# Transformer block on one core: tile 15's first output-projection half moved ahead of tiles 13 and 14's feed-forward, a last sum in 256 columns, and a fused last scaling

## The chip, the core and the metric

The kernel runs on one core of a Trainium2 chip. A core has a matrix engine (TensorE, PE in the profile), three engines for element-wise work (VectorE or DVE, ScalarE or ACT, GpSimd or POOL) and SyncE (SP), which here issues the data transfers. Each engine takes its instructions in the order of the program; engines wait for each other by semaphores. The metric is the device time of one execution in microseconds; several executions are timed and the median is given.

## The reference

One attention layer and one feed-forward layer with routed low-rank adapters, in float32, for 4 sequences of 512 tokens and 1024 features:

```python
x = x + layernorm(attention(layernorm(x)))       # 32 heads of 32, 8 KV heads, RoPE, causal
x = x + layernorm(feed_forward(layernorm(x)))

# end of attention:      out @ w_o.T + b_o
# feed_forward(h):       h @ base_w.T + base_b + 2 * sum over 2 of 8 experts of
#                        weight_e * (h @ lora_A[e].T) @ lora_B[e].T
# layernorm(v):          (v - mean(v)) / sqrt(var(v) + 1e-5), over the 1024 features
```

## The kernel before

**Tiles.** The 2048 tokens are 16 tiles of 128. Tiles are worked in the order 0 to 11, 13, 14, 15, 12, in pairs; the last pairs are (13, 14) and (15, 12). For a pair, a 1024x1024 projection is done by a seven-block Strassen form (`seven`, acc_q, acc_o, acc_f for q, o and f): seven blocks of four matmuls of 128x512, with sums of the two tiles' inputs (s_q, s_o, s_f) made on VectorE and GpSimd. The last pair's o and f are done a tile at a time by `whole`: for each half of 512 output columns, eight matmuls sum into one PSUM bank (f adds a ninth, the low-rank part, which reads lowT). Each weight block of 128x512 is a "piece" of 256 KB, loaded by SP into a ring of 13 (`bring_pieces`, L489); a slot is free again when all uses of its piece are done.

**A tile's way.** Attention: scores (sc), their maximum (nmax), exponentials (pr), scaling (pr by rtot, GpSimd), transposes (pt_p to prT), weighted values (av to aT). Then o of a tile: acc_o plus the bias into w (VectorE), bn_stats of each half (L511), aggregate (mv), veps, then on GpSimd rstd (L527, a power) and shift (L531, -mean x rstd); w is scaled by ScalarE or VectorE (L552, L546), added to y (the residual, loaded from x) and y is normed once more into w (`attended`). w is transposed (pt_h, L577, to T_h). T_h goes into the gate and low-rank product (acc_gl, L602) and into f; `gate` ranks the eight experts in a chain of small VectorE instructions, which ends in low, its transpose pt_low (L1224) and lowT. After f, `finished` takes w's statistics by halves, scales w, adds it to y and stores y (L1264). There are two y buffers: tile 15's y is loaded (L865) when tile 13's output has landed, tile 12's after tile 14's.

**Order.** The program does not leave the order to the hardware: a planner (`Order`) replays the kernel with a cost for each operation and writes every engine's instruction order. TensorE's lanes are scores, transposes, values and three dense lanes; in the dense lane `main_lane` projections stand in the order in which the code puts them there. At the end of the list:

```python
for n, pair in enumerate(pairs[:-1]):
    out_of(pair)
    if n + 2 < len(pairs):
        q_of(pairs[n + 2])
    ffn_of(pair)
for tok in pairs[-1]:
    out_of([tok])
for tok in pairs[-1]:
    ffn_of([tok])
```

So o of (13, 14) is followed by their f, then o of 15, o of 12, f of 15, f of 12. Between o and f of (13, 14) stand, on TensorE, the two tiles' transposes and gates and the last attention group of tile 12.

Of the kernel before, what the change touches and what calls it, by code (L numbers as in the profile page):

```python
# [16 lines left out]
P = 128  # L17
# [74 lines left out]
class Order:  # L92
# [173 lines left out]
def kernel(  # L266
# [228 lines left out]
    class Norm:  # L495


        def __init__(self, name, urgent):
            self.name, self.urgent = name, urgent
            self.stats = None  # L500

        def half(self, src, h):
            if self.stats is None:
                self.stats = small.tile(
                    [P, NH, 6], F32, tag="stats", bufs=4, name=f"stats_{self.name}"
                )
            cols = slice(h * 512, (h + 1) * 512)
            yield dve(
                0.69,
                self.urgent,  # L510
                lambda: nc.vector.bn_stats(out=self.stats[:, h, :], in_=src()[:, cols]),  # L511
            )

        def scale(self):
            name = self.name

            def aggr():
                self.mv = small.tile([P, 2], F32, tag="mv", bufs=4, name=f"mv_{name}")
                nc.vector.bn_aggr(out=self.mv, in_=self.stats)

            def eps():
                self.veps = small.tile([P, 1], F32, tag="veps", bufs=4, name=f"veps_{name}")
                nc.vector.tensor_scalar_add(self.veps, self.mv[:, 1:2], EPS)  # L523

            def root():
                self.rstd = small.tile([P, 1], F32, tag="rstd", bufs=4, name=f"rstd_{name}")
                nc.gpsimd.tensor_tensor(out=self.rstd, in0=self.veps, in1=neg_half, op=ALU.pow)  # L527

            def shift():
                self.shift = small.tile([P, 1], F32, tag="shift", bufs=4, name=f"shift_{name}")  # L530
                nc.gpsimd.tensor_scalar(  # L531
                    self.shift, self.mv[:, 0:1], self.rstd, -1.0, ALU.mult, ALU.mult
                )

            yield dve(0.2, self.urgent, aggr)
            yield dve(0.15, self.urgent, eps)
            yield pool(0.6, 0, root)
            yield pool(0.4, 0, shift)

        def apply(self, dst, src, h):  # L540
# [51 lines left out]
    def project(lhsT, w, n, name, needs, take):  # L592


        acc = []
        steps = []

        def issue(c):
            if not acc:
                acc.append(ps.tile([P, 512], F32, tag="ps", name=f"acc_{name}"))  # L600
            last = c == len(needs) - 1
            nc.tensor.matmul(  # L602
                acc[0][:, :n], lhsT=lhsT(c), rhs=w(c), start=(c == 0), stop=last
            )
            if last:
                start(take(acc[0], steps_of[c].done), order.now)

        for c in range(len(needs)):
            us = 0.858 if n == 512 else 0.24
            steps.append(Step(us, partial(issue, c), needs[c], bank=(c == 0)))  # L610
        steps_of = list(steps)
        return steps
# [4 lines left out]
            start(piece.used(step.done))  # L617
        return steps

    def whole(name, tok_name, k, lhsT, ready, take, room, used=None, more=None):  # L620

        used = used or block(name, plain, 0, k) + block(name, plain, 1, k)
        needs = [[ready[c // 4], used[c].here] for c in range(ND)]
        needs[0] += room
        if more:
            needs.append(more[2])
        return with_pieces(
            used,
            project(
                lambda c: lhsT()[:, c, :] if c < ND else more[0](),  # L630
                lambda c: used[c].sb if c < ND else more[1],
                512,
                f"{name}_{tok_name}_{k}",
                needs,
                take,
            ),
        )
# [608 lines left out]
    def finished(tok):  # L1246

        t = tok.t
        norm = Norm(f"4_{t}", 3)
        halves = [Task() for _ in range(NH)]  # L1250
        added, out_halves = [Task() for _ in range(NH)], [Task() for _ in range(NH)]

        def ended(h):
            yield from norm.half(lambda: tok.w, h)
            halves[h].finish(order.at)

        def out_half(h):
            yield from norm.apply(lambda: tok.w, lambda: tok.w, h)
            yield from add_half(lambda: tok.y, lambda: tok.w, h, 2, tok.last)
            added[h].finish(order.at)  # L1260
            cols = slice(h * 512, (h + 1) * 512)
            yield sp(
                0.7,
                lambda: nc.sync.dma_start(  # L1264
                    out=out[t * P : (t + 1) * P, cols], in_=tok.y[:, cols]
                ),
            )
            yield LANDS
            out_halves[h].finish(order.at)

        def rest():
            yield halves
            yield from norm.scale()
            for h in range(NH):
                start(out_half(h), order.at)
            yield added
            w_slots.give(order.at)
            yield out_halves
            y_slots.give(order.at)

        start(rest())
        return ended

    def ffn(pair):

        ended = [finished(tok) for tok in pair]

        def to(k, h):
            return pair[k].w[:, h * 512 : (h + 1) * 512]

        def free(k, at):
            hT_slots.give(at)

        def lowT(k):
            return lambda: pair[k].lowT

        lo, hi = wlora_sb[:, :512], wlora_sb[:, 512:D]
        if len(pair) == 2:
            a, b = pair
            d, has_d = [], Task()  # L1300

            def difference():
                yield [a.low_done, b.low_done]
                d.append(small.tile([P, P], F32, tag="lowTd", bufs=1, name=f"lowTd_{a.t}"))
                yield dve(0.2, 1, lambda: nc.vector.tensor_sub(d[0], a.lowT, b.lowT))
                has_d.finish(order.at)
# [20 lines left out]
        tok = pair[0]  # L1327

        def take(h, acc, done):
            yield done  # L1330
            if h == NH - 1:
                free(0, order.at)
            cols = slice(h * 512, (h + 1) * 512)
            yield dve(0.69, 0, lambda: nc.vector.tensor_add(to(0, h), acc, bbase_sb[:, cols]))
            banks.give(order.at)
            yield from ended[0](h)

        steps = []
        for h in range(NH):
            steps += whole(  # L1340
                "f",
                tok.t,
                h,
                tok.hT_tile,
                tok.h_ready,
                partial(take, h),
                [],
                more=(lowT(0), (lo, hi)[h], [tok.low_done, loaded["lora"]]),
            )
        return steps  # L1350
# [269 lines left out]
    def out_of(pair):  # L1620
        main_lane.extend(attention_out(pair))
# [15 lines left out]
        for steps in products:  # L1637
            main_lane.extend(steps[k * ND : (k + 1) * ND])
    q_of(pairs[1])
    for n, pair in enumerate(pairs[:-1]):  # L1640
        out_of(pair)
        if n + 2 < len(pairs):
            q_of(pairs[n + 2])
        ffn_of(pair)
    for tok in pairs[-1]:
        out_of([tok])
# [80 lines left out]
```

## Time and profile before

| | us |
|---|---|
| median of 3 runs (1186.48 to 1186.75) | 1186.6 |
| the profiled execution | 1187.52 |
| its span in the trace | 1185.7 |
| TensorE busy, of the span | 1145.5 (97%) |
| VectorE busy | 823.9 (69%) |
| mean granted TensorE clock | 0.994 of full |

The span is the time from the first to the last instruction in the trace; the rest of an execution's time lies around it. A row of a timeline gives start, busy time, engine, line, operation, result<-inputs, shapes and count. TensorE's matmuls are pipelined: a row's busy time has about 0.15 us of a last matmul's way through the array in it, so the pace is read from one start to the next. TensorE's idle time by who ended it, from 1060 us on (us in total, times, longest):

```profile
PE pt_h L577 <- DVE rtot L1422: 5.9, 1, 5.9
PE acc_f L602 <- ACT lowT L335: 0.4, 1, 0.4
PE pt_low L1224 <- DVE low L1212: 0.4, 1, 0.4
PE acc_o L602 <- DMA piece<-in_w_o_dram: 0.3, 1, 0.3
```

### The profile page before, as it was taken

The numbers are of one execution on the slowest core, as the hardware profiler recorded it, in microseconds if no ns is written. First come the engines' busy times: TensorE is split into PE (matmuls) and PEld (weight loads), VectorE is DVE, ScalarE is ACT, GpSimd is POOL, SyncE is SP. The second block draws the span as 40 slices with busy tenths as digits, with TensorE's granted clock in tenths as the row PEclk, the third lists the DMA queues.
The fourth block names the chain that finished last, engine by engine and source line by source line (L and its number), as shares of the span: only waits on it lengthen the run. The fifth ranks groups of instructions, "written<-read, shape, count | busy, mean of one in ns | idle before, by whom it ended". The sixth has DMA issues, their size and how long they took to land.

```text
span 1185.7 us, 21412 instructions
## 1 busy us (share of the span) xinstructions
PE 1145.5 (97%) x7248; PEld 627.0 (53%) x7248; DVE 823.9 (69%) x1609; ACT 533.1 (45%) x1555; POOL 608.0 (51%) x857
## 2 busy tenths in 40 slices
PE   7999999999999999999999999999999999998996
PEld 3445545555556555565545555556655555545443
DVE  4687877875778756787667775678866786675353
ACT  0355544555555345454524334456543554552010
POOL 2575866553656536456455444545544564544221
PEclk9999999999999999999999999999999999998998
DMA  9869768434672636635377344762457645573883
GB/s 347 292 233 350 248 216 264 152 124 152 218 253 74 195 119 226 206 108 174 120 244 244 126 160 143 226 210 81 161 179 244 214 134 164 168 267 110 284 303 110
DMA packets 118315, 232.52 MB, mean 196 GB/s; under 512 B 13504, under 2 KB 14528, under 8 KB 118208
## 3 DMA queue, kind: packets, MB, share of 16 engines
q1 hardware_dynamic: 118208, 231.16, 59.0%
q8 instruction: 58, 0.95, 0.3%
q14 instruction: 49, 0.40, 0.1%
HBM read 210.14 MB, written 20.97 MB: 195 GB/s over the span
## 4 chain that ended last, share of the span: by engine, by line
PE 80%; DVE 8%; DMA 4%; POOL 4%; ACT 2%; issue 1%; SPq 0%; POOLq 0%; ACTq 0%; DVEq 0%
PE acc_f L602 19%; PE acc_o L602 15%; PE acc_q L602 11%; PE pt_p L1467 11%; PE acc_kv L602 7%; PE sc L1372 6%; PE av L1490 6%; PE acc_gl L602 2%; DVE nmax L1451 2%; POOL pr L1407 2%; ACT pr L1393 1%; PE pt_h L577 1%; DVE sc L1441 1%; DMA mix_o<-in_w_o_dram 1%; PE pt_q L996 1%
## 5 line engine op out<-in xcount | busy, mean ns | idle before, releaser
L1407 POOL TENSOR_SCALAR pr<-pr,rtot 128x256 f32<-128x256 f32 (+3 forms) x512 | 303.9, 610 | 249.3 <-DVE rtot L1422 183.9
L1393 ACT ACTIVATE pr<-sc,nmax 128x256 f32<-128x256 f32 (+3 forms) x512 | 264.6, 537 | 108.7 <-DVE nmax L1451 60.8
L1451 DVE TENSOR_REDUCE nmax<-sc 128x2 f32<-128x768 f32 (+3 forms) x176 | 198.2, 1126 | 32.6 <-ACT pr L1393 28.7
L1467 PE MATMUL pt_p<-ident,pr 128*128 128x128 f32 x1280 | 174.2, 276 | 3.5 <-POOL pr L1407 1.6
L1467 PEld LDWEIGHTS pt_p<-ident,pr 128*128 128x128 f32 x1280 | 144.1, 141 | 61.4 <-issue 46.5
L335 ACT COPY prT<-pt_p 128x512 f32<-128x512 f32 (+1 forms) x264 | 135.2, 548 | 83.6 <-PE pt_p L1467 82.9
L1441 DVE TENSOR_TENSOR sc<-sc,cmask 128x256 f32<-128x256 f32 (+2 forms) x176 | 96.7, 549 | 41.0 <-PE sc L1372 35.0
L602 PE MATMUL acc_kv<-wkv_sb,T_xn 128*128 128x512 f32 x256 | 119.4, 600 | 0.0
L335 ACT COPY aT<-av 128x128 f32<-128x128 f32 (+2 forms) x82 | 25.6, 312 | 195.0 <-PE av L1490 195.0
L1393 ACT ACTIVATION_READ_ACCUMULATOR pr<-sc,nmax 128x1 f32 x512 | 108.9, 213 | 0.0
L602 PE MATMUL acc_f<-piece,T_h 128*128 128x512 f32 x232 | 108.7, 596 | 0.0
L602 PE MATMUL acc_o<-piece,aT 128*128 128x512 f32 x232 | 106.3, 595 | 0.5 <-DMA piece<-in_w_o_dram 0.3
L602 PE MATMUL acc_q<-piece,s_q 128*128 128x512 f32 x224 | 105.1, 597 | 1.2 <-DVE raw_q L713 0.9
L602 PE MATMUL acc_o<-piece,s_o 128*128 128x512 f32 x224 | 103.4, 593 | 0.7 <-PE av L1490 0.7
L602 PE MATMUL acc_f<-piece,s_f 128*128 128x512 f32 x224 | 103.6, 593 | 0.0
L602 PE MATMUL acc_q<-piece,T_xn 128*128 128x512 f32 x224 | 102.7, 594 | 0.0
L343 POOL TENSOR_TENSOR y<-y,w 128x512 f32<-128x512 f32 x62 | 80.1, 1307 | 29.5 <-ACT w L552 15.1
L1372 PE MATMUL sc<-kT,qT 32*128 32x384 f32 (+3 forms) x1024 | 93.9, 464 | 0.6 <-ACT pr L1393 0.6
L527 POOL TENSOR_TENSOR rstd<-veps,neg_half 128x1 f32<-128x1 f32 x64 | 35.2, 554 | 114.5 <-DVE veps L523 114.2
L1490 PEld LDWEIGHTS av<-prT,v 128*32 128x32 f32 x2560 | 64.5, 109 | 49.8 <-issue 39.3
L1490 PE MATMUL av<-prT,v 128*32 128x128 f32 x2560 | 88.1, 276 | 0.0
L336 DVE COPY prT<-pt_p 128x512 f32<-128x512 f32 (+1 forms) x88 | 56.2, 641 | 32.2 <-PE pt_p L1467 31.5
(151 smaller groups left out, 1406.5 us busy)
## 6 DMA issues: line engine op xcount, KB each, us to landing
piece<-in_w_o_dram SPq DMA_DIRECT2D x116, 256.0 KB, 3.8
piece<-in_w_base_dram SPq DMA_DIRECT2D x116, 256.0 KB, 3.3
piece<-mixed_q SPq DMA_DIRECT2D x112, 256.0 KB, 3.5
piece<-mixed_o SPq DMA_DIRECT2D x112, 256.0 KB, 4.3
piece<-mixed_f SPq DMA_DIRECT2D x112, 256.0 KB, 3.4
piece<-in_w_qkv_dram SPq DMA_DIRECT2D x100, 256.0 KB, 3.7
xa<-in_x_dram SPq DMA_DIRECT2D x32, 256.0 KB, 4.1
y<-in_x_dram SPq DMA_DIRECT2D x16, 512.0 KB, 5.3
```

The lines of the kernel that those rows point to most:

```text
L335: act=(0.15 + n * 0.00085, lambda: nc.scalar.copy(out(), in_())),
L336: dve=(0.15 + n * 0.00105, lambda: nc.vector.tensor_copy(out(), in_())),
L343: engine.tensor_tensor(out=out(), in0=in0(), in1=in1(), op=op)
L527: nc.gpsimd.tensor_tensor(out=self.rstd, in0=self.veps, in1=neg_half, op=ALU.pow)
L602: nc.tensor.matmul(acc[0][:, :n], lhsT=lhsT(c), rhs=w(c), start=(c == 0), stop=last)
L1372: nc.tensor.matmul(sc[:, r, c * n : (c + 1) * n], lhsT=tok.qT[g.kt][rows, (g.at + c) % GROUP, :], rhs=seq.kT[g.kt][rows, :n], start=True, ...
L1393: lambda: nc.scalar.activation(pr[:, c * n : (c + 1) * n], sc4[:, r, c, :], AF.Exp, bias=nmax[:, r, c : c + 1], accum_out=total[:, r, c : ...
L1407: lambda: nc.gpsimd.tensor_scalar(pr[:, c * n : (c + 1) * n], pr[:, c * n : (c + 1) * n], rtot[:, r, c : c + 1], 1.0, ALU.mult, ALU.mult,),
L1441: lambda: nc.vector.tensor_tensor(out=diag, in0=diag, in1=cmask.unsqueeze(1).unsqueeze(1).to_broadcast([P, q, g.n, P]), op=ALU.add,),
L1451: lambda: nc.vector.tensor_reduce(nmax[:, some, : g.n], sc4[:, some], AX.X, ALU.max, negate=True),
L1467: nc.tensor.transpose(pt[:, j, :], g.pr[r][:, j * P : (j + 1) * P], ident)
L1490: nc.tensor.matmul(av[r * HD : (r + 1) * HD, c, :], lhsT=g.seq.v[j][:, head * HD : (head + 1) * HD], rhs=g.prT[r][:, c * (i + 1) + j, :], ...
```

## The change

Three parts:

1. `out_of([15])` is split: its first half (eight matmuls, columns 0 to 511) goes into `main_lane` ahead of `ffn_of((13, 14))`, the second half stays behind it. The pieces' loads follow the order of `main_lane`.
2. f of tile 12 (the last tile) is done in four sums of 256 columns in place of two of 512. The two sums of a half use the same eight pieces, one sum after the other. Bias add and bn_stats are done by quarters, and the aggregate takes four groups.
3. In the last tile, VectorE makes y = w x rstd + y for a half in one `scalar_tensor_tensor` as soon as rstd is there, and ScalarE adds shift to it. Scaling w and adding it to y were two instructions before, behind shift.

```diff
+    out_of(pairs[-2])
+    late, behind = pairs[-1]
+    at = len(main_lane)
+    out_of([late])
+    first_half, second_half = main_lane[at : at + ND], main_lane[at + ND :]
+    del main_lane[at:]
+    main_lane.extend(first_half)
+    ffn_of(pairs[-2])
+    main_lane.extend(second_half)
+    out_of([behind])
     for tok in pairs[-1]:
         ffn_of([tok])
...
         def out_half(h):
-            yield from norm.apply(lambda: tok.w, lambda: tok.w, h)
-            yield from add_half(lambda: tok.y, lambda: tok.w, h, 2, tok.last)
+            cols = slice(h * 512, (h + 1) * 512)
+            y = tok.y[:, cols]
+            if tok.last:
+                yield dve(
+                    0.75,
+                    0,
+                    lambda: nc.vector.scalar_tensor_tensor(
+                        y, tok.w[:, cols], norm.rstd, y, ALU.mult, ALU.add
+                    ),
+                )
+                yield shifted
+                yield act(
+                    0.65,
+                    0,
+                    lambda: nc.scalar.activation(y, y, AF.Identity, bias=norm.shift),
+                )
+            else:
+                yield from norm.apply(lambda: tok.w, lambda: tok.w, h)
+                yield from add_half(lambda: tok.y, lambda: tok.w, h, 2)
             added[h].finish(order.at)
...
         def rest():
-            yield halves
-            yield from norm.scale()
+            yield quarters if tok.last else halves
+            start(scaled(), order.at)
+            yield rooted if tok.last else shifted
             for h in range(NH):
                 start(out_half(h), order.at)
...
+        def take_quarter(k, acc, done):
+            yield done
+            cols = slice(k * 256, (k + 1) * 256)
+            yield dve(
+                0.42,
+                0,
+                lambda: nc.vector.tensor_add(tok.w[:, cols], acc[:, :256], bbase_sb[:, cols]),
+            )
+            banks.give(order.at)
+            yield from ended[0](k)
+
         steps = []
+        if tok.last:
+            for h in range(NH):
+                used = block("f", plain, 0, h, 2) + block("f", plain, 1, h, 2)
+                for q in range(2):
+                    steps += whole(
+                        "f",
+                        tok.t,
+                        h,
+                        tok.hT_tile,
+                        tok.h_ready,
+                        partial(take_quarter, 2 * h + q),
+                        [],
+                        used,
+                        (lowT(0), (lo, hi)[h], [tok.low_done, loaded["lora"]]),
+                        slice(q * 256, (q + 1) * 256),
+                    )
+            return steps
```

`quarter` is `half` with 256 columns and a statistics tile of four groups; `scale` takes `rooted`, a task that it finishes between rstd and shift; `whole` takes `cols`, the columns of a piece that its matmuls read; `ended_quarter` is what `finished` returns for the last tile, and `scaled` runs `scale` and then finishes `shifted`.

More of the change, by code (lines that the diff above doesn't have):

```diff
@@ L500, in __init__, with quarter @@
             self.stats = None
+        def quarter(self, src, k):
+            if self.stats is None:
+                self.stats = small.tile(
+                    [P, 2 * NH, 6], F32, tag="stats4", bufs=1, name=f"stats_{self.name}"
+                )
+            cols = slice(k * 256, (k + 1) * 256)
+            yield dve(
+                0.4,
+                self.urgent,
+                lambda: nc.vector.bn_stats(out=self.stats[:, k, :], in_=src()[:, cols]),
+            )
         def half(self, src, h):
@@ L512, in half, with scale @@
             )
-        def scale(self):
+        def scale(self, rooted=None):
             name = self.name
@@ L537, in scale @@
             yield pool(0.6, 0, root)
+            if rooted:
+                rooted.finish(order.at)
             yield pool(0.4, 0, shift)
@@ L608, in project @@
         for c in range(len(needs)):
-            us = 0.858 if n == 512 else 0.24
+            us = {512: 0.858, 256: 0.432}.get(n, 0.24)
             steps.append(Step(us, partial(issue, c), needs[c], bank=(c == 0)))
@@ L618, in with_pieces, with whole @@
         return steps
-    def whole(name, tok_name, k, lhsT, ready, take, room, used=None, more=None):
+    def whole(name, tok_name, k, lhsT, ready, take, room, used=None, more=None, cols=None):
         used = used or block(name, plain, 0, k) + block(name, plain, 1, k)
@@ L630, in whole @@
                 lambda c: lhsT()[:, c, :] if c < ND else more[0](),
-                lambda c: used[c].sb if c < ND else more[1],
-                512,
-                f"{name}_{tok_name}_{k}",
+                lambda c: (used[c].sb if c < ND else more[1])[:, cols or slice(0, 512)],
+                cols.stop - cols.start if cols else 512,
+                f"{name}_{tok_name}_{k}" + (f"_{cols.start}" if cols else ""),
                 needs,
@@ L1251, in finished @@
         added, out_halves = [Task() for _ in range(NH)], [Task() for _ in range(NH)]
+        quarters, rooted, shifted = [Task() for _ in range(2 * NH)], Task(), Task()
         def ended(h):
@@ L1255, in ended, with ended_quarter @@
             halves[h].finish(order.at)
+        def ended_quarter(k):
+            yield from norm.quarter(lambda: tok.w, k)
+            quarters[k].finish(order.at)
         def out_half(h):
-            yield from norm.apply(lambda: tok.w, lambda: tok.w, h)
-            yield from add_half(lambda: tok.y, lambda: tok.w, h, 2, tok.last)
+            cols = slice(h * 512, (h + 1) * 512)
[17 more added lines that the diff above has]
+                yield from add_half(lambda: tok.y, lambda: tok.w, h, 2)
             added[h].finish(order.at)
-            cols = slice(h * 512, (h + 1) * 512)
             yield sp(
@@ L1264, in out_half @@
                 lambda: nc.sync.dma_start(
-                    out=out[t * P : (t + 1) * P, cols], in_=tok.y[:, cols]
+                    out=out[t * P : (t + 1) * P, cols], in_=y
                 ),
@@ L1269, in out_half, with scaled @@
             out_halves[h].finish(order.at)
+        def scaled():
+            yield from norm.scale(rooted)
+            shifted.finish(order.at)
         def rest():
-            yield halves
-            yield from norm.scale()
+            yield quarters if tok.last else halves
+            start(scaled(), order.at)
+            yield rooted if tok.last else shifted
             for h in range(NH):
@@ L1281, in finished @@
         start(rest())
-        return ended
+        return ended_quarter if tok.last else ended
     def ffn(pair):
@@ L1336, in take @@
             yield from ended[0](h)
-        steps = []
+        def take_quarter(k, acc, done):
+            yield done
+            cols = slice(k * 256, (k + 1) * 256)
+            yield dve(
+                0.42,
+                0,
+                lambda: nc.vector.tensor_add(tok.w[:, cols], acc[:, :256], bbase_sb[:, cols]),
+            )
+            banks.give(order.at)
+            yield from ended[0](k)
+        steps = []
+        if tok.last:
[13 more added lines that the diff above has]
+                        slice(q * 256, (q + 1) * 256),
+                    )
+            return steps
         for h in range(NH):
@@ L1639 @@
     q_of(pairs[1])
-    for n, pair in enumerate(pairs[:-1]):
+    for n, pair in enumerate(pairs[:-2]):
         out_of(pair)
@@ L1644 @@
         ffn_of(pair)
-    for tok in pairs[-1]:
-        out_of([tok])
+    out_of(pairs[-2])
[8 more added lines that the diff above has]
+    out_of([behind])
     for tok in pairs[-1]:
```

## The prediction

> **What bounds the kernel now.** I read the page's busy shares first, then TensorE's idle times from about 1060 us to the end, then those stretches by engine and granted clock, and last the chain of waits through the final ten microseconds.
>
> ```profile
> PE 1145.5 (97%) x7248; PEld 627.0 (53%) x7248; DVE 823.9 (69%) x1609; ACT 533.1 (45%) x1555; POOL 608.0 (51%) x857
> ```
>
> TensorE sets the time. A change that leaves its work alone can only win idle time, time at a low clock, or what follows the last matmul. Before tile 13's transposes the first two are found together. Timeline of TensorE (start, busy time, group, count, idle before it and what ended that; an fp32 matmul leaves two records, a transpose one):
>
> ```profile
> 1063.59 1.13 PE L602 MATMUL acc_o<-piece,aT 128*128 128x512 f32 x2
> 1070.61 2.23 PE L577 MATMUL pt_h<-ident,w 128*128 128x128 f32 x8 [5.90 <-DVE rtot L1422]
> 1072.63 2.03 PE L602 MATMUL acc_gl<-wgl_sb,T_h 128*128 128x136 f32 x8
> 1074.45 1.91 PE L602 MATMUL acc_f<-piece,T_h 128*128 128x512 f32 x2
> 1080.69 1.04 PE L577 MATMUL pt_h<-ident,w 128*128 128x128 f32 x8
> 1086.38 3.60 PE L602 MATMUL acc_f<-piece,s_f 128*128 128x512 f32 x8
> ```
>
> The idle before tile 13's pt_h is named after rtot, but pt_h reads w: it waits for tile 13's two layer norms on VectorE and GpSimd. The eight transposes then take 2.23 us, against 1.04 us for tile 14's. By stretch (the number after POOL's is the granted clock, then the DMA engines' busy share):
>
> ```profile
> 1066.00:1068.00 2.00, 0.00 (x0) 0.00 (x0) 1.59 (x6) 2.00 (x14) 0.47 (x2) 1.00 0.34 121
> 1068.00:1070.00 2.00, 0.00 (x0) 0.00 (x0) 0.43 (x5) 1.56 (x10) 2.00 (x6) 0.91 0.00 0
> 1070.00:1072.00 2.00, 1.36 (x6) 0.99 (x7) 1.25 (x4) 1.52 (x2) 2.00 (x5) 0.50 0.00 0
> 1074.00:1076.00 2.00, 2.00 (x5) 1.13 (x5) 1.13 (x4) 0.00 (x0) 1.95 (x6) 0.50 0.00 0
> 1076.00:1078.00 2.00, 2.00 (x11) 1.42 (x10) 0.52 (x3) 0.16 (x1) 1.95 (x6) 0.88 0.24 75
> ```
>
> The clock falls to half some 5 us into the idle (0.91 as a mean of 1068 to 1070) and is full again at about 1076.5. The end, from the chain of waits:
>
> ```profile
> 1176.56 0.70 DVE w L1334
> 1177.29 0.70 DVE stats L511
> 1178.02 0.22 DVE mv L519
> 1178.26 0.16 DVE veps L523
> 1178.49 0.56 POOL rstd L527
> 1179.14 0.28 POOL shift L531
> 1179.44 0.82 ACT w L552
> 1180.29 1.60 DVE y L343
> ```
>
> Here everything is serial. The last add takes 1.60 us beside GpSimd's add of the other half, where the same add on VectorE took 0.69 us alone (w<-w,w at 1103.73).
>
> **Part 1: tile 15's first o half moves up.** It is eight matmuls. In the dense stretch from 1091.80, 44 records took 18.89 us, 0.429 each, so the block is 16 x 0.429 = 6.87 us of TensorE, spent at 1110.52 today. In the changed program it stands between pairs (13,14)'s last o matmul and tile 13's pt_h. Today's stretch from the end of that o matmul (1063.59 + 2 x 0.429 = 1064.45) to acc_f_1 at 1086.38 is 21.93 us. Its work at full clock: two pt_h of 0.87 (start of 1138.25 to 1139.12), two acc_gl of 1.85 (1139.98 to 1141.83), four acc_f_0 matmuls 3.43, 16 pt_p transposes 1.74, av_4 1.02 (1084.10 to 1085.12), pt_low 0.11: 11.74 us. So 10.19 us is lost: 5.90 idle, some 3 to half clock, the rest waits.
>
> Can the block start at 1064.45? In the built order only its eighth matmul waits for ScalarE, whose copy of the last aT chunk ends at 1065.71; the seventh ends near 1070.5, so that wait is covered. Its weights take the places in SP's queue that eight f pieces have now, issued between 1048.48 and 1056; the median landing is 3.8 us. The PSUM banks and w's buffer are long free (tile 11's y add ended at 1060.96). I take a start at 1064.45 and an end at 1071.32. pt_h's inputs are ready at 1070.5 and 1071.7, so it follows at once, and at full clock, as TensorE has not idled.
>
> What queues behind it: VectorE's order has the block's bias add (0.69) ahead of the T_h copy and tile 15's bn_stats (0.69) among tile 14's. Replayed by the rows' durations, the add ends at 1072.24, the T_h copies (one now ScalarE's, 0.59) at 1072.6 and 1073.1: TensorE waits 0.4 us before acc_gl. From there nothing waits: pr_1 is scaled by 1075.1 (TensorE wants it at 1075.3), tile 14's w is ready at 1077.9, two more pr scalings of 0.36 ahead of its rstd on GpSimd counted (wanted 1078.75), the prT copies at 1081.4 (av wants 1081.9), s2 of the Strassen sums at 1082.55 (wanted 1083.45). One sum moves from GpSimd to VectorE (1.27 off, 0.69 to 1.75 on); the gate chain behind it delivers low of tile 14 at 1088.1, wanted at 1088.6. Slack is 0.2 to 1 us at each; contention between VectorE and GpSimd (0.69 against 1.75 on s_f rows) could cost up to 1 us over all. With the 0.4, acc_f_1 starts at 1064.45 + 6.87 + 11.74 + 0.4 = 1083.46: 2.92 us earlier, and the 6.87 is gone from later. **Part 1: -9.79 us.**
>
> SP: the eight loads now precede 28 f pieces. The ring has 13 slots, so five f pieces are in when the block starts, and the other eight of acc_f_0 to acc_f_3's first follow as it frees slots, 0.86 us each, with the DMA engines at 0.34 and 0.00 in the stretches above. All are in by 1076, before they are wanted. So the loads cost nothing; without that idle DMA they would arrive as late as 1110 to 1131 shows, some 0.5 us. What is late next: tile 15's y. Its load waits for tile 13's output and is issued 5.3 us after the f block; landing took at most 5.4 us; its add now wants it 10.85 us after. That is level, with 0.6 us of slack to the next add in VectorE's order and 1.75 more before pt_h. I charge nothing.
>
> The o blocks: TensorE waits about 0.5 us for pieces at the 22nd to 24th matmul after the f block (the y loads block SP). pt_h now falls before the 24th and covers its 0.28. **-0.28 us.**
>
> **Part 2: 256 columns.** 18 matmuls become 36. Records of 136 columns start 1.85/16 = 0.116 us apart, of 512 0.429: by interpolation 0.216 for 256, 72 x 0.216 against 36 x 0.429, +0.09. Every record reloads its weights; at 136 columns the loads (about 0.12 each) are already hidden, so these should be. [...]
>
> A wait is added: pt_low now stands directly before the matmul that reads lowT. For tile 15 the same adjacency gave pt_low at 1148.70 and its reader at 1149.38, 0.68 where 0.11 is work. Today tile 12 covers it with two matmuls. **+0.57.** Eight pieces are held for two passes; the last three are issued behind tile 15's two outputs, at about 5.5 us into this block, and wanted from 10.6 on: covered.
>
> The last bias add falls from 0.69 to 0.41 (the 128x256 add of L924), bn_stats by as much, an estimate (bounds 0 and -0.35): **-0.56** together.
>
> **Part 3: the end.** From rstd to the second output's issue now: 1182.29 (two issues of 0.38 from 1181.91) less 1179.05, 3.24 us. After: VectorE y = w x rstd + y, first half, 0.69 (no such row at 512 columns; bounds 0.55, the scaling row, and 1.60, the contended add; it is nearest to the plain add, as GpSimd then runs only the 0.28 us shift), then ScalarE's shift, two in a row 0.72 apart and 0.81 long (1070.15 and 1070.87): 0.03 + 0.69 + 0.03 + 0.72 + 0.81 + 0.02 = 2.30. **-0.94** (bounds -1.1 and -0.0).
>
> **The sum.** -9.79 - 0.28 + 0.09 + 0.57 - 0.56 - 0.94 = -10.9 us. Span 1185.7 to 1174.8; 1.82 us lie around it (that execution took 1187.52). The median of 1186.6 is 0.9 below that execution: 1186.6 - 10.9 = **1175.7 us**.
>
> **The rivals.**
> - *Partial fill.* The block waits for aT from its first matmul (1.3 us), or VectorE's longer queue stalls TensorE by about as much. For: slacks under 1 us, in-order engines. Against: the built order. 1177.0 to 1178.
> - *The clock stays low.* If the half clock has a cause other than the idle, its 3.1 us stay: 1178.8. Against: it falls 5 us into the idle and nowhere else in this stretch.
> - *Loads show* in part 2: 36 x 0.12 (1.81 us for 15 loads at 136 columns) = 4.3 us: 1180.0.
> - *It doesn't do what it says:* the moved block is itself late (its pieces behind SP), the idle stays, only the end is won, about 0.8: 1185.8. Against: the pieces' issue times.
> - *Slower:* at 256 columns no load hides, all 72 records pay up to 0.19 us (the load's busy time in 512-column rows): 13.7 us, so 1189.4. It decides from 0.15 us a record (10.9/72). Against: the acc_gl rows again.
>
> **Chances.** Forecast 0.70, partial fill 0.14, clock 0.05, loads 0.04, not done 0.04, slower 0.03. The measurement tells about 0.2% (2.4 us) from no change. So faster 0.93, same 0.04, slower 0.03. Range: below, no waits and the best prices, 1174.3; above, the first two rivals, 1179.0.
>
> **What would show it.** Right: pt_h of tile 13 straight behind acc_o at about 1071.3, clock 1.00 there, acc_f_1 near 1083.5, the next acc_o starting on its second half near 1107.7; about 0.7 us from pt_low to its reader in tile 12; 256-column records 0.216 apart; 2.3 us from rstd to the last issue. Wrong: idle before the moved block or between it and acc_f_1, a clock of 0.50, or a wait for y of tile 15.

## The result, and the profile after

| | before | changed |
|---|---|---|
| median of six runs each, us | 1186.67 (1185.19 to 1189.75) | 1176.88 (1175.27 to 1179.10) |
| ratio, 95% interval | | 0.9917 [0.9901, 0.9933] |
| the profiled execution, us | 1187.52 | 1178.71 |
| its span, us | 1185.7 | 1177.1 |
| mean granted TensorE clock | 0.994 | 0.999 |

The change makes the kernel 9.8 us faster by the medians (the interval is 8.0 to 11.7). Timed twice more, beside other kernels, it came to 0.9911 [0.9896, 0.9926] and 0.9924 [0.9908, 0.9940]. The forecast was 1175.7 us, in a range from 1174.3 to 1179.0.

A single execution must not be set against another by its span alone. The point where pair (13, 14)'s o ends, up to which TensorE's instructions are as before, came at 1065.64, 1061.77 and 1064.02 us in three profiled executions of the same changed program. From there to the end of the span those three took 111.46, 110.93 and 110.98 us. So most of the variation between runs lies ahead of that point, and every comparison below is made from the start of the last `acc_o` row of pair (13, 14): 1063.59 before, 1065.64 after.

TensorE's timeline in the changed kernel, from there to the transposes of tile 15 (start, busy time, group, count, idle before it and what ended it):

```profile
1065.64 7.99 PE L618 MATMUL acc_o<-piece,aT 128*128 128x512 f32 x18
1073.46 1.04 PE L593 MATMUL pt_h<-ident,w 128*128 128x128 f32 x8
1074.74 2.12 PE L618 MATMUL acc_gl<-wgl_sb,T_h 128*128 128x136 f32 x16 [0.24 <-ACT T_h L335]
...
1086.06 3.60 PE L618 MATMUL acc_f<-piece,s_f 128*128 128x512 f32 x8
...
1110.20 18.19 PE L618 MATMUL acc_o<-piece,aT 128*128 128x512 f32 x42
1128.63 1.98 PE L618 MATMUL acc_o<-piece,aT 128*128 128x512 f32 x4 [0.24 <-DMA piece<-in_w_o_dram]
1130.45 1.04 PE L593 MATMUL pt_h<-ident,w 128*128 128x128 f32 x8
```

The first row now has 18 records in place of two: the moved block follows without a gap, and tile 13's `pt_h` follows the block. The transposes take 1.04 us where they took 2.23. The stretches around them (the number after POOL's is the granted clock):

```profile
1068.00:1070.00 2.00, 2.00 (x6) 0.84 (x5) 1.59 (x6) 2.00 (x14) 0.42 (x2) 1.00 0.81 256
1070.00:1072.00 2.00, 2.00 (x6) 0.95 (x5) 0.43 (x5) 1.61 (x10) 2.00 (x6) 1.00 0.86 288
1074.00:1076.00 2.00, 1.76 (x15) 1.53 (x14) 1.82 (x4) 0.59 (x1) 2.00 (x2) 1.00 0.85 283
```

The clock is full from 1060 us to the last matmul, and TensorE is busy in stretches in which it was idle or at half speed. What TensorE still waits for from 1055 us on (us in total, times, longest):

```profile
PE acc_f L618 <- ACT lowT L335: 0.4, 1, 0.4
PE acc_f L618 <- DVE lowT L336: 0.4, 1, 0.4
PE acc_gl L618 <- ACT T_h L335: 0.2, 1, 0.2
PE acc_o L618 <- DMA piece<-in_w_o_dram: 0.2, 1, 0.2
```

The 5.9 us are gone. The second row is new: the wait for tile 12's lowT in the last block, whose start looks so:

```profile
1153.00 3.62 PE L618 MATMUL acc_f<-piece,T_h 128*128 128x256 f32 x16
1156.46 0.27 PE L1241 MATMUL pt_low<-ident,low 128*128 128x128 f32 x1
1157.11 0.70 PE L618 MATMUL acc_f<-wlora_sb,lowT 128*128 128x256 f32 x2 [0.39 <-DVE lowT L336]
```

From `pt_low` to its reader 0.65 us pass; the 16 records of 256 columns ahead of it start 3.46/16 = 0.216 us apart. And the end, all engines:

```profile
1169.51 0.42 DVE L1389 TENSOR_TENSOR w<-acc_f,bbase_sb 128x256 f32<-128x256 f32 x1 [3.00 <-PE acc_f L618]
1169.96 0.43 DVE L512 BATCH_NORM_STATS2 stats<-w 128x6 f32<-128x256 f32 x1
...
1170.96 0.55 POOL L541 TENSOR_TENSOR rstd<-veps,neg_half 128x1 f32<-128x1 f32 x1 [13.05 <-DVE veps L537]
1171.54 1.42 DVE L1288 SCALAR_TENSOR_TENSOR y<-w,rstd,y 128x512 f32<-128x512 f32 x2 [0.66 <-POOL rstd L541]
1171.60 0.82 POOL L545 TENSOR_SCALAR shift<-mv,rstd 128x1 f32<-128x1 f32 x1
1172.46 1.33 ACT L1296 ACTIVATE y<-y,shift 128x512 f32<-128x512 f32 x2 [16.42 <-POOL shift L545]
1173.20 0.95 SPq L1304 DMA_DIRECT2D out_dram<-y  x2
```

Both halves' multiply-adds stand on VectorE directly behind rstd, and ScalarE adds shift to each. Laid end to end, the stretches give the whole difference:

| stretch, by what starts it | before, us | after, us | difference | forecast |
|---|---|---|---|---|
| last acc_o of (13, 14) to acc_f_1, moved block taken out of after (6.87) and counted below | 22.79 | 13.55 | -9.24 | -9.79 |
| acc_f_1 to the next acc_o | 24.14 | 24.14 | 0 | 0 |
| acc_o to pt_h of tile 15, before without the moved 6.87 | 20.86 | 20.25 | -0.61 | -0.28 |
| pt_h of tile 15 to f of tile 12 | 22.55 | 22.55 | 0 | 0 |
| f of tile 12 to the last bias add | 15.76 | 16.51 | +0.75 | +0.66 |
| last bias add to the aggregate | 1.46 | 0.92 | -0.54 | -0.56 |
| aggregate to rstd's end | 1.02 | 1.08 | +0.06 | 0 |
| rstd's end to the second output's issue | 3.30 | 2.31 | -0.99 | -0.94 |
| that issue to the end of the span | 3.36 | 3.28 | -0.08 | 0 |
| sum | | | -10.65 | -10.9 |

(In the first row 22.79 is 1086.38 less 1063.59, and 13.55 is 1086.06 less 1065.64 less 6.87. The forecast's 0.66 is its 0.09 and 0.57.)

### The profile page after: what moved, and what is told of

It reads as the page before. It is cut to its first block, busy times and chain, and to the rows that moved or that the text cites. A ratio compares the mean times of both kernels' runs of the same rounds, so it can differ in the third digit from the quotient of the medians.

```text
span 1177.1 us, 21495 instructions
## 1 busy us (share of the span) xinstructions
PE 1142.5 (97%) x7284; PEld 631.8 (54%) x7284; DVE 820.2 (70%) x1613; ACT 534.2 (45%) x1557; POOL 606.1 (51%) x855
## 4 chain that ended last, share of the span: by engine, by line
PE 77%; DVE 8%; DMA 7%; POOL 4%; ACT 2%; issue 1%; SPq 1%; POOLq 0%; ACTq 0%; DVEq 0%
PE acc_f L618 19%; PE acc_o L618 15%; PE pt_p L1541 10%; PE acc_q L618 10%; PE sc L1446 6%; PE av L1564 6%; PE acc_kv L618 5%; DVE nmax L1525 2%; PE acc_gl L618 2%; ACT pr L1467 2%; DMA mix_f<-in_w_base_dram 2%; POOL pr L1481 2%; DVE sc L1515 1%; DMA piece<-in_w_qkv_dram 1%; DMA xa<-in_x_dram 1%
## 5 line engine op out<-in xcount | busy, mean ns | idle before, releaser
L618 PE MATMUL acc_f<-piece,T_h 128*128 128x512 f32 (+1 forms) x264 | 108.0, 541 | 0.0
```

Source lines behind the costliest of these rows:

```text
L618: nc.tensor.matmul(acc[0][:, :n], lhsT=lhsT(c), rhs=w(c), start=(c == 0), stop=last)
```

## The experiments

Each was timed against the kernel before on the same chip; ratios are to that kernel. Trace comparisons go from the last `acc_o` row of pair (13, 14), as above.

**The move alone.** The kernel before with part 1 of the change and nothing else.

```diff
-    for n, pair in enumerate(pairs[:-1]):
+    for n, pair in enumerate(pairs[:-2]):
...
-    for tok in pairs[-1]:
-        out_of([tok])
+    out_of(pairs[-2])
+    late, behind = pairs[-1]
+    at = len(main_lane)
+    out_of([late])
+    first_half, second_half = main_lane[at : at + ND], main_lane[at + ND :]
+    del main_lane[at:]
+    main_lane.extend(first_half)
+    ffn_of(pairs[-2])
+    main_lane.extend(second_half)
+    out_of([behind])
```

> Part 1 of the change alone (the moved half; the last tile as before). Theory (the move fills TensorE's idle and keeps its clock): nearly the whole gain, about 9.9 us from before: from the start of pair (13,14)'s last o matmul to acc_f_1 20.4 us as with the whole change (22.8 before), clock 1.00 throughout, 0.4 us or less idle there. Rival (the end contributes a large share): 5 us or less.

Measured: 1177.74 us, ratio 0.9922 [0.9907, 0.9938]. From acc_o (1063.00) to acc_f_1 (1083.42) the run took 20.42 us, as the changed kernel did, and in all 10.3 us less than before. There was no wait for a piece in its o stretch, which took 19.74 us. So part 1 makes nearly all of the gain.

**The end alone.** The changed kernel with the old order of blocks, so parts 2 and 3 without part 1.

```diff
-    for n, pair in enumerate(pairs[:-2]):
+    for n, pair in enumerate(pairs[:-1]):
...
-    out_of(pairs[-2])
...
-    out_of([behind])
+    for tok in pairs[-1]:
+        out_of([tok])
```

> Parts 2 and 3 alone (256 columns and the fused end; tile 15's o where it was). Theory: about 0.8 us faster than before, inside the noise; the 5.9 us idle and the half clock are there again. By stretches: tile 12's f 0.7 to 0.8 us longer, last add and bn_stats 0.54 shorter, rstd to the second output's issue 2.3 us instead of 3.24. Rival (the end contributes a large share): 4 us or more.

Measured: 1185.82 us, ratio 0.9986 [0.9973, 0.9999]. The trace is 1.69 us shorter than before. Of this 0.73 belongs to no edit: from acc_o to acc_f_1 the run took 22.06 us, since its half clock ended sooner after the work resumed (the last section has both edges). Another 0.14 lies in the o stretch; 0.82 is left for parts 2 and 3. The idle is back, and so is the slow transpose; TensorE's row from that run:

```profile
1069.69 2.23 PE L593 MATMUL pt_h<-ident,w 128*128 128x128 f32 x8 [5.88 <-DVE rtot L1496]
```

**The clock without the gain.** The kernel before, with five matmuls of 512 columns that nobody reads in the place where the change puts the o block. They fill some of the idle, but take no work from later.

```diff
+    def keep_busy(n):
...
+            nc.tensor.matmul(
+                acc[0], lhsT=ident, rhs=bo_sb[:, :512], start=(c == 0), stop=(c == n - 1)
+            )
...
+        if pair is pairs[-2]:
+            keep_busy(5)
```

> The kernel before, with five matmuls of 128x512 added behind pair (13,14)'s o whose sum nobody reads: TensorE is busy for 4.3 us of the idle, and no work of the kernel is moved. Theory (the clock falls because of the idle): clock 1.00 throughout; pt_h of tile 13 starts when it did, 7.0 us after the last o matmul's start, but acc_f_1 comes about 3 us earlier than before (19.8 us after that start, 22.8 before); about 3 us faster in all. So 3 of the change's 10 us are clock and 7 are idle. Rival (the clock falls for another reason, as the transposes or the gate products): no gain, pt_h still 2.2 us for eight transposes.

Measured: 1187.09 us, ratio 0.9992 [0.9983, 1.0002], where about 3 us less than before were expected: the timing can't tell it from nothing. In the trace the run is about 1.9 us shorter from acc_o to the end (120.2 against 122.1). TensorE's rows of this run, and two stretches with the clock:

```profile
1066.02 4.46 PE L1646 MATMUL acc_busy<-bo_sb,ident 128*128 128x512 f32 x10
1072.07 0.63 PE L577 MATMUL pt_h<-ident,w 128*128 128x128 f32 x4 [1.59 <-DVE rtot L1422]
1073.18 0.66 PE L577 MATMUL pt_h<-ident,w 128*128 128x128 f32 x4 [0.49 <-ACT w L552]
```

```profile
1070.00:1072.00 2.00, 0.47 (x2) 0.00 (x0) 0.62 (x3) 1.43 (x7) 2.00 (x6) 1.00 0.00 0
1072.00:1074.00 2.00, 1.45 (x11) 1.24 (x12) 1.26 (x4) 1.13 (x2) 2.00 (x4) 1.00 0.00 0
```

The transposes start 7.01 us after acc_o began, as before (7.02), so the norms set that point. The clock stays full over 1.59 us of idle, and the rival that gave the half clock another cause is out. This is one execution: its mean clock was 0.998, and in the eleven timed ones it lay between 0.994 and 0.998 (0.993 to 0.996 before), so some of them may still have had a stretch at half clock. acc_f_1 comes 20.46 us after acc_o, 2.33 us earlier than before, where 3 was expected: at full speed the second half of the transposes has to wait 0.49 us for its w, which half speed had covered. Later 0.9 us of wait for an o piece (0.3 before) gives part of the gain back. So of the change's 9.24 us, 5.9 are the idle and 2.3 the clock; the other 1.0 is small waits.

**Both halves ahead.** If half of tile 15's o fills the idle, the rest of it might shorten what still waits. The changed kernel with all 16 of its o matmuls ahead of the feed-forward of (13, 14).

```diff
     out_of([late])
-    first_half, second_half = main_lane[at : at + ND], main_lane[at + ND :]
-    del main_lane[at:]
-    main_lane.extend(first_half)
     ffn_of(pairs[-2])
-    main_lane.extend(second_half)
     out_of([behind])
```

> The change with both halves of tile 15's o ahead of the pair's feed-forward, sixteen matmuls instead of eight. Theory (only idle time and clock are won, and 0.24 us of idle is left after the change): no further gain, within 1 us of the change; TensorE has no idle there, acc_f_1 comes 6.9 us later and the o stretch is 6.9 us shorter. Rival (o earlier, or its weights fetched while the DMA engines are idle, is what gains): 3 us or more faster than the change.

Measured: 1180.83 us, ratio 0.9948 [0.9935, 0.9962], 4 us slower than the change. Both expectations missed. TensorE's rows behind the feed-forward of (13, 14), and the load of tile 15's y and GpSimd's rows in the same time:

```profile
1114.98 13.90 PE L618 MATMUL acc_o<-piece,aT 128*128 128x512 f32 x32
1132.41 0.66 PE L593 MATMUL pt_h<-ident,w 128*128 128x128 f32 x4 [3.54 <-DVE w L562]
1133.62 1.12 PE L593 MATMUL pt_h<-ident,w 128*128 128x128 f32 x4 [0.55 <-ACT w L568]
```

```profile
1120.77 0.33 SPq L882 DMA_DIRECT2D y<-in_x_dram  x1
1125.44 2.48 POOL L343 TENSOR_TENSOR y<-y,w 128x512 f32<-128x512 f32 x2 [0.93 <-ACT w L568]
1130.46 1.06 POOL L541 TENSOR_TENSOR rstd<-veps,neg_half 128x1 f32<-128x1 f32 x2 [2.53 <-DVE veps L537]
```

The idle has moved: it is now tile 15's norms that TensorE waits for. The y buffers are two, so tile 15's y load follows tile 13's output and was issued at 1120.77. It landed 4.4 us later, at about 1125.2; the adds begin on GpSimd at 1125.44, as the scaled w that their row names came no earlier than 1125.36. The second norm's rstd is made from 1130.46 on. In the change 20.2 us of o stood in between as cover; here it is 13.7. The clock falls again (0.50 in the stretch from 1134 to 1136). Whether late y or the in-order engines made the wait was open; the run with an own y, below, tells it apart.

**The change again, as a base.** The same program on the chip of the next three runs.

> The change itself, once more and on the same chip as the three runs beside it, as their base. From the first timing: 0.9917 of the kernel before, about 1177 us, with the f block's start 20.4 us behind the start of the last acc_o matmul of pair (13,14).

Measured: 1174.71 us, ratio 0.9911 [0.9896, 0.9926]; 20.42 us to acc_f_1. There was no wait for a piece in the o stretch (0.24 in the first profile).

**Without the quarters.** The changed kernel, its last f block in 512 columns as before.

```diff
-            yield quarters if tok.last else halves
+            yield halves
...
-        return ended_quarter if tok.last else ended
+        return ended
...
-        if tok.last:
-            for h in range(NH):
...
-            return steps
```

> The change without its part 2: the last f block in 512 columns and halves, as before; the moved o block and the fused end stay. Theory (part 2 gains 0.5 us on VectorE behind the last matmul and gives 0.8 back on TensorE in front of it): f of tile 12 takes 15.7 us instead of 16.5, the last add and its bn_stats 1.46 us instead of 0.92, from rstd's end to the second output's issue 2.3 us in both. In all 0.2 to 0.3 us faster than the change, which a timing can't tell from nothing; the stretches can. Rival (the quarters pay, since the wait for lowT would also arise with halves): f of tile 12 stays at 16.2 us or more, and the kernel is 0.5 us slower than the change.

Measured: 1175.67 us, ratio 0.9914 [0.9900, 0.9927], no difference in the timing. By stretches: f of tile 12 15.76 us against 16.50 in the base, last add to aggregate 1.46 against 0.92. So part 2 gives 0.54 us at the end, loses 0.74 in front of it and 0.06 in the wider aggregate, and costs about 0.26 net. The theory holds by these stretches; from acc_o to the end the run took no less than the base (110.94 against 110.93 us), as it waited some 0.35 us for an o piece ahead of them.

**The low-rank matmul later.** The wait for lowT arises because its reader stands right behind `pt_low`; here the reader moves some matmuls on, in both of the last blocks.

```diff
+            steps.insert(ND + 5, steps.pop(ND))
             return steps
...
+        steps.insert(ND + 2, steps.pop(ND))
         return steps
```

> The change, with the low-rank matmul of the last two f blocks issued some matmuls later: in tile 12's blocks behind pt_low and two or more matmuls of the next group, in tile 15's behind the other half's first ones. Theory (TensorE waits 0.4 us for lowT only because its reader stands directly behind pt_low): neither wait is left, f of tile 12 takes 15.9 us instead of 16.5, pt_h of tile 15 to f of tile 12 22.1 us instead of 22.55; in all 1.0 us faster than the change, the best version so far. Rival (lowT is late whatever stands between, or the longer held PSUM banks and the first column groups ending later make a new wait): no more than 0.2 us faster, and a wait for a bank, or the last group's add queued behind another add.

Measured: 1175.62 us, ratio 0.9910 [0.9895, 0.9925]: not better than the change. Neither wait for lowT is left, and from pt_h of tile 15 to f of tile 12 the run took 21.88 us (22.56 in the base, 22.1 expected). But f of tile 12 took 16.61 us. A new wait stands in it; TensorE's row, and the load queue's in that block:

```profile
1161.37 1.17 PE L618 MATMUL acc_f<-piece,T_h 128*128 128x256 f32 x4 [0.45 <-DMA piece<-in_w_base_dram]
```

```profile
1153.99 0.34 SPq L1304 DMA_DIRECT2D out_dram<-y  x1
1154.43 0.38 SPq L489 DMA_DIRECT2D piece<-in_w_base_dram  x1
1155.22 0.34 SPq L1304 DMA_DIRECT2D out_dram<-y  x1
1155.65 0.88 SPq L489 DMA_DIRECT2D piece<-in_w_base_dram  x2
```

Tile 15's two outputs both go ahead of the last three pieces in the change; now the second stands between the first piece and the other two, and the pieces took 5.7 us to land in place of 3.7 (medians of three). The first was issued 4.1 us into the block and not 5.4, and still one of them landed too late. The rival's time came, no gain, but not by the waits that it named (a bank, a queued add): a transfer that looked covered became the bound. A further 1.50 us went in the o stretch, in a wait for an o piece; there the load order is the change's, and the landing was 6.7 us against 5.0 in the base. Over the runs that place these loads the same way this wait was 0, 0, 0, 0.24, about 0.35 and 1.50 us. Up to there every engine's instructions and all loads stand in the base's order, so it is chance, and not this edit's doing.

**Both halves, with an own y for tile 15.** The slow kernel above, but tile 15's y goes into the buffer of the x tiles, which is free by then, so its load waits only until tile 14's y has landed.

```diff
-        yield y_slots.take()
+        own = tok.t == T - 1
+        if own:
+            yield tok.before.has_y
+            yield xa_slots.take()
+        else:
+            yield y_slots.take()
...
+            if own:
+                tok.y = xpool.tile([P, D], F32, tag="xa", bufs=1, name=f"y_{tok.t}")
+            else:
+                tok.y = xpool.tile([P, D], F32, tag="y", bufs=2, name=f"y_{tok.t}")
...
-            y_slots.give(order.at)
+            if tok.t != T - 1:
+                y_slots.give(order.at)
```

> Both halves of tile 15's o ahead of f of tiles 13 and 14, as in the run that came 4 us behind the change, and tile 15's y in a buffer of its own (that of the x tiles, free by then), so that its load need not wait for tile 13's output. Theory (that run's idle of 3.5 and 0.5 us before tile 15's pt_h, and the low clock behind it, came from tile 15's late y): the load is issued before f(13,14), pt_h of tile 15 follows o(12) with less than 0.3 us of idle at clock 1.00, and the time is within 1 us of the change. Rival (13.7 us of o(12) is too short a cover for the norm whenever y comes, as its instructions stand behind others in VectorE's and GpSimd's order): the idle before pt_h stays above 2 us, and the time 3 to 4 us above the change.

Measured: 1173.50 us, ratio 0.9899 [0.9883, 0.9914]; the interval overlaps the base's. Tile 15's y was issued at 1044.03. TensorE's rows:

```profile
1097.60 1.04 PE L593 MATMUL pt_h<-ident,w 128*128 128x128 f32 x8
...
1115.89 13.90 PE L618 MATMUL acc_o<-piece,aT 128*128 128x512 f32 x32
1129.62 7.03 PE L618 MATMUL acc_f<-piece,T_h 128*128 128x512 f32 x16
```

With y early, tile 15's transposes (1097.60) run inside the feed-forward of (13, 14), so o of tile 12 has nothing to cover for them and f of tile 15 follows it at once. The 3.54 and 0.55 us are gone: they hung on the late y, since the two kernels differ in its buffer alone, and in the order that the planner makes of that. How much of them the in-order engines had added (with y late, tile 15's statistics ended at 1128.65 and their aggregate came at 1129.52, behind a bias add of tile 12) is not parted. From acc_o to the end the run took 109.56 us, against 110.93 in the base and 115.23 with the late y.

**The own y without the second half.** The changed kernel with the edit to y alone.

> The change, with nothing but tile 15's y moved to a buffer of its own; one half of tile 15's o moves up, as in the change. It tells apart what made the run with both halves and an own y the fastest. Theory A (the own buffer frees the load queue: in the change SP stands still for 3 us on the y load of tile 12, which waits for tile 14's output, and the three o pieces behind it then land just before or after they are wanted; with an own y for tile 15 that load waits for tile 13's output, earlier): o_1 of tile 15 and o of tile 12 take 19.7 us with no wait for a piece (0 to 1.5 us in the four runs so far that place them so), nothing else moves, and the time is 0 to 0.5 us below the change. Theory B (the second half matters: it takes tile 15's transposes and its low-rank turn into f(13,14), and with them the 0.41 us wait for tile 15's lowT): that wait is still here, and from the last acc_o of pair (13,14) to the end this takes about 0.9 us more than the 109.6 of the run with both halves. Both can hold.

Measured: 1175.33 us, ratio 0.9909 [0.9894, 0.9924], the same as the change; 110.82 us from acc_o to the end. The o stretch took 19.74 us with no wait, but so it did in the base run, so theory A's gain is at most the chance wait it takes away, and nothing here shows more. Theory B holds: the wait for tile 15's lowT (0.41) and that for T_h (0.24 of idle) are still here, and neither is in the run with both halves. That run is 1.26 us shorter, where 0.9 was expected.

**The best of them together.** Both halves up, the own y, and only the second half of the last block cut into 256 columns.

```diff
+            steps += whole(
+                "f", tok.t, 0, tok.hT_tile, tok.h_ready, take_first, [], more=more[0]
+            )
+            used = block("f", plain, 0, 1, 2) + block("f", plain, 1, 1, 2)
+            for q in range(2):
...
+                    partial(take_quarter, 2 + q),
```

> Both halves of tile 15's o up, tile 15's y in an own buffer, and the 256 columns for the second half of the last f block only; its first half is one sum of 512 columns again. Theory (part 2's cost is the wait for lowT behind pt_low in the first quarter, its gain is at the very end, so only the second half need be cut): pt_low stands two matmuls ahead of its reader again and no wait is left there, f of tile 12 takes 15.9 us instead of 16.4, the last add and bn_stats 0.92 us as with four quarters; 0.4 us less than the run with both halves and own y, and so about 1.6 us less than the change: ratio to before near 0.9895, which a timing can't tell from 0.9899, but the two stretches can. Rival (the held pieces of the second half, or VectorE's four sums of statistics in another order, bring a new wait): f of tile 12 above 16.2 us, or more than 0.2 us between the last matmul's end and the last add.

Measured: 1173.75 us, ratio 0.9901 [0.9883, 0.9918]: the timing can't tell it from the run with both halves and an own y, as expected. TensorE's rows at the start of the last block:

```profile
1146.81 5.31 PE L618 MATMUL acc_f<-piece,T_h 128*128 128x512 f32 x12
1151.96 0.27 PE L1249 MATMUL pt_low<-ident,low 128*128 128x128 f32 x1
1152.07 1.88 PE L618 MATMUL acc_f<-piece,T_h 128*128 128x512 f32 x4
```

`pt_low` again has two matmuls (four records) between it and its reader, and in this run no wait of TensorE is left from 1055 us to the end. f of tile 12 to the last add took 15.81 us, against 16.50, and from acc_o to the end 108.85. The theory holds, with 0.7 us where 0.4 was expected.

To see whether that gain is real, this kernel and the change were timed side by side:

> The change a third time, as the base of the run beside it: 0.991 to 0.992 of the kernel before, and in the trace about 111 us from the last acc_o of pair (13,14) to the end of the span.

> The fastest version so far (both halves of tile 15's o up, own y for tile 15, 256 columns in the second half of the last block only) on the same chip as the change. Theory: the 2.1 us that its trace is shorter from the last acc_o of pair (13,14) to the end (108.85 against 110.93) are its gain; ratio to before 0.989 to 0.990, 0.0018 below the change's. Rival: what is won there is lost ahead of that point, where the load order differs too; then both ratios are within 0.0008.

Measured: the change 1177.16 us, ratio 0.9924 [0.9908, 0.9940]; the other 1175.12 us, ratio 0.9904 [0.9886, 0.9922]. The medians are 2.0 us apart, and the traces 2.1 (110.98 and 108.88 us from acc_o to the end). The two intervals still overlap, so the size rests on the traces, which agree in both pairs.

## Why the prediction was right

The sum was 10.9 us; the trace has 10.65, the two later traces of the change 11.2 and 11.1 (122.11 us before, 110.93 and 110.98 after, from acc_o to the end), and the three timings 9.8, 11.5 and 8.7 (differences of medians). That 10.65 lies so near is partly luck: 0.55 too much in part 1 is more than half made up by 0.33 too little in the o blocks. Point by point, as the table above has it:

- **The idle and the clock (part 1).** Right in mechanism, 0.55 us too large. The block ran from the end of the last acc_o with no gap, the 0.4 us wait for T_h came as replayed (0.41 from the transposes' end to acc_gl), and nothing else waited. The missing 0.55 lies in changes from one group to the next: six of 0.06 to 0.14 us each, for which the list of work at full clock (11.74 us) had no term. The clock run parts the 9.24 into 5.9 of idle, 2.3 of clock, where the prediction had some 3, and 1.0 of small waits.
- **Not one of the queue's risks came true.** The loads came in time. Tile 15's y was issued 5.3 us after the o block began and added at 10.84 us, as worked out, with no wait for it. The prediction called it level, by a longest landing of 5.4 us. In this run the load took 4.0 us and was in 1.5 us before its add. But 5.4 was read from the transfers behind 1100 us, loads and stores together, and the sixteen y loads of the kernel before took 3.6 to 8.9 us. With 8.9 the add would have come some 3.4 us late, so charging nothing went well in part by luck. Where the run with both halves ahead takes 6.9 us of this cover away, the late y does turn into 3.5 us of idle.
- **The o blocks.** -0.61 against -0.28. In part this is chance: the same program had 0 or 0.24 us of wait there.
- **256 columns.** The records stand 0.216 us apart, the number that was interpolated, so no loads show: the 16 weight loads from 1152.89 on (3.33 us) lie beside the 16 records that start 3.46/16 us apart. Both rivals that hung on the loads, 1180.0 and 1189.4, are out.
- **lowT.** The new wait came where it was put, +0.75 for the block against +0.66. The last add and bn_stats gained 0.54 against 0.56. So part 2 was charged 0.10 net and cost 0.26; the run without it confirms that it does not pay in this form.
- **The end.** -0.99 against -0.94, but two errors cancel in it. ScalarE began 0.95 us after rstd and not 0.75, since it waited for shift, which took 0.82 us on GpSimd and not 0.28. Its two additions then took 1.33 us and not 1.53. The second issue before was at 1182.34 us, not at the 1182.29 that the forecast starts from; with it the forecast would have been -1.00.

Of the rivals, *partial fill* came nearest in time (1177 to 1178), but not in its mechanism: there was no idle ahead of the block or in it, and behind it only the 0.41 us that the sum had. *The clock stays low* fell with the clock run. What moved the median up to 1176.88 in the first timing, against 1175.7, is within what runs of the same program differ by (1174.71 and 1177.16 in the other two).

## What to carry to other kernels

Work that is ready early and needed late is good cover for an idle stretch of the engine that sets the time; take just so much of it that what it covered before stays covered, or first make early what that cover was for (here a residual tile that waited for a buffer: by the traces 4 us slower with it late, 1.4 us faster with it early). A last sum that is cut up to shorten the tail moves its operands' deadline forward too, so only the piece at the very end should be cut, and a matmul that reads a just-made operand kept some matmuls behind it (that took both waits for lowT away, though the run that did only this lost as much to loads). Where runs differ by as much as an edit is worth, compare two traces from a point that the edit does not touch.

## What the runs showed of the hardware

**The half clock lasted once or twice 3.41 us.** Three of the runs had a stretch at half clock ahead of their last matmul. Quarter-microsecond stretches around its two edges (the number after POOL's is the granted clock) give its length; first the kernel before, then the end-alone run, then that with both halves and the late y:

```profile
1069.50:1069.75 0.25, 0.00 (x0) 0.00 (x0) 0.00 (x0) 0.06 (x1) 0.25 (x2) 0.79 0.00 0
1076.25:1076.50 0.25, 0.25 (x3) 0.25 (x2) 0.00 (x0) 0.00 (x0) 0.25 (x2) 0.55 0.00 0
```

```profile
1067.25:1067.50 0.25, 0.00 (x0) 0.00 (x0) 0.19 (x2) 0.25 (x4) 0.25 (x2) 0.56 0.00 0
1074.00:1074.25 0.25, 0.25 (x1) 0.00 (x0) 0.21 (x2) 0.00 (x0) 0.25 (x2) 0.78 0.00 0
```

```profile
1133.00:1133.25 0.25, 0.07 (x1) 0.00 (x0) 0.14 (x1) 0.25 (x1) 0.25 (x1) 0.97 0.89 295
1136.50:1136.75 0.25, 0.25 (x2) 0.18 (x1) 0.22 (x2) 0.00 (x0) 0.00 (x0) 0.70 1.06 410
```

The stretches between these edges read 0.50, those just outside 1.00. A mean of 0.79 over 0.25 us is then 0.105 us at half, so in the first the clock fell at 1069.65 and rose at 1076.48, after 6.83 us. In the second it fell at 1067.28 and rose at 1074.11, 6.83 again; in the third the two are 1133.24 and 1136.65, 3.41. So the half clock lasted two, two and one times 3.41 us. The falls came 4.9, 3.5 and 4.4 us after the idle began; in the third work had resumed 0.8 us before. The next fall came behind the last matmul; its rows, in the same three runs:

```profile
1178.75:1179.00 0.25, 0.00 (x0) 0.00 (x0) 0.00 (x0) 0.00 (x0) 0.25 (x1) 0.74 0.00 0
```

```profile
1179.75:1180.00 0.25, 0.00 (x0) 0.00 (x0) 0.00 (x0) 0.07 (x1) 0.00 (x0) 0.84 0.00 0
```

```profile
1174.00:1174.25 0.25, 0.00 (x0) 0.00 (x0) 0.25 (x1) 0.00 (x0) 0.25 (x1) 0.89 0.00 0
```

By these rows the clock fell 102.39, 105.81 and 37.55 us after it had risen. Divided by half of the 6.83 us, 3.415, that is 29.98, 30.98 and 11.00, within 0.02 of whole numbers; no run shows what sets these lengths. What an idle costs differs from run to run, by when the clock falls and rises: TensorE's instructions are the same up to the idle in the first two, yet the fall came 6.06 us after acc_o began in the one and 4.60 in the other. The first had 5.87 us of resumed time at half speed, the second 4.42, and half of that difference is the 0.73 us by which the end-alone run was quicker without any edit for it.

**A tiny GpSimd instruction three times as long.** shift on 128x1 took 0.27 us before and 0.82 in the changed kernel, where it runs beside VectorE's two multiply-adds (0.71 each). The run without the quarters has 0.82 too, and in eight other runs with part 3 GpSimd's step between rstd and ScalarE's addition took 0.88 or 0.89 us (0.89 here). The rows of the kernel before, where the tiles lie in SBUF and TensorE's sums in PSUM: of its 64 shifts, 62 took 0.27 or 0.28 us, among them one at 756.90 that lies wholly inside VectorE's w<-acc_o,bo_sb, with one input in PSUM; the two others, 0.40 at 158.78 and 0.33 at 539.90, ran beside turn_k<-raw_k,rope_sb, with both inputs in SBUF, as y = w x rstd + y has them. But one at 1162.00, beside the last 0.15 us of above<-above,tied on 128x64, both in SBUF too, took 0.28. No run took the multiply-adds away with shift kept in place, so the cause is not shown; the delay of ScalarE, about 0.2 us, is in the rows.

**A landing time is no constant.** Three o pieces issued back to back behind the load of tile 12's y took 5.0, 5.4 and 6.7 us (medians) to land in three runs with the same load order, and TensorE waited 0, 0.24 and 1.50 us for them.
